# Spectral pieces beside the selective scan: transfers issued by ScalarE in the place of SyncE, four columns mixed in one piece, at most four pieces a step

## The chip, the cores and the metric

The kernel runs on one core of one Trainium2 chip. The metric is the device time of one execution in microseconds; the time of the kernel before is the median of three runs. The profile is of one further execution.

Engine names are those of the profile: PE is the matrix engine (TensorE), PEld its weight loads, DVE is VectorE, ACT is ScalarE, POOL is GpSimd, SP is SyncE, which only issues transfers here. PEclk is the clock that was granted to PE, as a share of full speed.

## The reference

The input x is (8, 64, 64, 96): eight images of 64 × 64 positions with 96 channels, in 32-bit floats. Four residual layers follow one another; each normalizes its input in groups of three channels over the whole image and adds its result to x:

```python
x = x + L0(_gn(x))   # selective scan: 4 orders of the 4096 positions, 192 channels, 16 states each
x = x + L1(_gn(x))   # chunked scan of the same 4 orders with one decay per head
x = x + L2(_gn(x))   # selective scan as L0, with other weights
x = x + L3(_gn(x))   # spectral layer
```

The core of a selective scan is, per position of an order,

```python
h = h * exp(dt * A) + (dt * u) * b      # 192 channels x 16 states
y = sum_n(h * c)
```

The spectral layer raises the image to 128 × 128 with a low-pass filter, applies to each of the 16384 positions a hidden layer of 384 with the polynomial c0 + c1·h + c2·h², comes back to 96 channels, filters again and keeps every second row and column. The filters are separable, so the kernel writes them as products with the matrices `up` (64 to 128) and `down` (128 to 64), first along one direction, then along the other.

## The kernel before

**The images.** A loop goes over the eight images. For each, L0, L1 and L2 are computed one after the other with `project`, the scan and `back`. The spectral layer of an image needs little of DVE and POOL, so it isn't computed at its own place but in small pieces beside the two selective scans of the next image: the first half beside L0's, the second half beside L2's. The first image has no pieces beside it. The last image's spectral layer is done at the end in `spectral_layer`, which the change does not touch. So 14 of 16 selective scans have pieces beside them.

**The scan.** `selective_scan` goes over 32 steps (four orders of eight chunks of 512 positions). A step has six units t, n = t % 6; a unit is 32 channels × 4 states on the partitions and four groups of states along the free axis. The order of all instructions is written out by hand (`manual_schedule`): each engine and each transfer queue takes its instructions in the order in which the program issues them. For one unit:

- `spread` (L834, PE): `pu`, the channels of dt·u repeated over the partitions, into the one buffer `misc`;
- `with_b` (L840): `db` = pu · b, on DVE; for n = 2 and 5 on POOL instead, from the loaded `du2`;
- `decays(t, p)` (L855, ACT): `da` = exp(dt · A), half p of the unit into one of two buffers, which is free again only when the scan of the same half of the unit before has read it;
- `scan(t, p)` (L870, DVE): the recurrence over half p, into `h`;
- `leave` (L886 ACT, L891 POOL): the last state is copied out, then h is multiplied by c in place. `enter` (L826, ACT) puts the state where the scan three units on starts from;
- `total_y` (L898 and L908, PE): sums h over its states into `py`, for the units 0 to 2 of a step in unit 3, for 3 to 5 in unit 0 of the next step; ACT copies the sums to y (L993 in unit 4, L1007 in unit 1).

`prepare` works up to two steps ahead: it makes dt, b, c and du of a chunk (PE L742 and L751, ACT L747, L755 and L775, POOL L793 or L799), writes them to DRAM and loads them back repeated over partitions (`bcd`, `dd`, `dud`, `dx`, `b`, `c`, `du2`). All these transfers are issued by SP.

**The pieces.** `slow_layer` makes two lists of pieces. A piece is a tuple (load, norm, matmuls, evacuation, store, lead). The three kinds are:

- `rows(j)`, 16 of two pieces: normalize and turn four rows, then multiply by `up` and store to `x1d`. One load of `xs` (the tile sx) serves two j.
- `cols(n)`, 32 of seven pieces: load four columns of x1d (the tile sc), multiply by `up` (`down_h`, `fine` L509); three times `hidden` and `square` (L516, L523); two `mix` pieces of two columns each (L532 and L536, evacuated by `mixed` L547); `lower` (L555, L564) and a store to `g2d`.
- `ends(j)`, 16 of one piece: load `xr` (the tile sr, once for two j) and `g2` (the tile s) from g2d, add the bias (`shift`, L588), multiply by `down`, add the residual (L592 and L601), evacuate (`done`, L611), store to the output.

The first list has the rows, two empty places and the columns 0 to 14: 139 places. The second has the columns 15 to 31, two empty places and the ends: 137.

**Beside.** The class `Beside` puts the lists into the scan. `begin` issues a piece's matmuls into a PSUM buffer that it shares with total_y and prepare (`py`) or with spread (`misc`). `end` issues the evacuation on ACT, then the loads that are due, and the `norm` of the next piece. A store isn't issued by `end` but kept in `waiting`, and `flush` issues it when the next piece has begun. A load is issued when the piece before its own is next, at the earliest. All loads and stores of the pieces go through SP, in the order of the program, between those of `prepare`.

Each step has a quota: list length times step number over 32, rounded down, less the same for the step before; here four or five pieces. The text calls the places in a step A to E: A begins and ends in unit 1, B begins at the start of unit 2 and ends in its middle, C begins there and ends at the unit's end, D lies in the first half of unit 4, E at the start of unit 5.

Of the kernel before, what the change touches and what calls it, by code (L numbers as in the profile page):

```python
# [17 lines left out]
DM = 96  # L18
# [49 lines left out]
def tile_vision_stack(  # L68
# [19 lines left out]
    nc = tc.nc  # L88
# [55 lines left out]
    w2q, b1q, coefq = hidden_parts(w3bs)  # L144
# [288 lines left out]
    def slow_layer(prev):  # L433
# [12 lines left out]
        def rows(j):  # L446

            def load():
                if j % 2 == 0:
                    live["xs", j] = xs = wide("sx")[:DM]  # L450
                    nc.sync.dma_start(xs, xd[:, j * 256 : j * 256 + 512])

            def norm():
                if j % 2 == 0:
                    live["xn"] = xn = wide("sn")[:DM]
                    nc.scalar.activation(
                        xn, live["xs", j], AF.Identity, scale=sb[:, 0:1], bias=sb[:, 1:2]
                    )

            def turn(ps):  # L460
                pt = ps[:64, : 4 * DM].rearrange("p (i c) -> p i c", i=4)
                for i in range(4):
                    at = (j % 2) * 256 + 64 * i
                    nc.tensor.transpose(pt[:, i, :], live["xn"][:, at : at + 64], ident[:DM, :DM])

            def turned(ps):
                live["xt"] = xt = narrow("st", "g")
                nc.scalar.copy(xt[:64].rearrange("p i c -> p (i c)"), ps[:64, : 4 * DM])

            def across(ps):  # L470
                nc.tensor.matmul(
                    ps[:, : 4 * DM],
                    up,
                    live["xt"][:64].rearrange("p i c -> p (i c)"),
                    start=True,
                    stop=True,
                )

            def crossed(ps):
                live["x1"] = x1 = wide("sw")[:, : 4 * DM]  # L480
                nc.scalar.copy(x1, ps[:, : 4 * DM])

            def store():
                nc.sync.dma_start(
                    x1d[4 * j : 4 * j + 4].rearrange("h w c -> w h c"),
                    live["x1"].rearrange("p (h c) -> p h c", h=4),
                )

            return [(load, norm, turn, turned, None, 4), (None, None, across, crossed, store, 0)]

        def cols(n):

            def load():
                live["c1"] = c1 = narrow("sc", "x1")[:64]
                nc.sync.dma_start(c1, x1d[:, 4 * n : 4 * n + 4])

            def down_h(ps):
                for i in range(4):
                    nc.tensor.matmul(
                        ps[:DM, i * 128 : i * 128 + 128],  # L500
                        live["c1"][:, i, :],
                        up,
                        start=True,
                        stop=True,
                    )

            def fine(ps):
                live["x2"] = x2 = wide("s2")[:DM]
                nc.scalar.copy(x2, ps[:DM])  # L509
                live["f"] = []  # L510

            ops = [(load, None, down_h, fine, None, 4 if n else 0)]
            for m in range(3):

                def hidden(ps, m=m):
                    nc.tensor.matmul(  # L516
                        ps, w3as[:, m * 128 : (m + 1) * 128], live["x2"], start=True, stop=True
                    )

                def square(ps, m=m):  # L520
                    f = wide("sf")
                    live["f"].append(f)
                    nc.scalar.activation(f, ps, AF.Square, bias=b1q[:, m : m + 1])  # L523

                ops.append((None, None, hidden, square, None, 0))
            for p in range(2):

                def mix(ps, p=p):
                    for i in range(2):
                        at = (2 * p + i) * 128  # L530
                        po = ps[:, i * DM : i * DM + DM]
                        nc.tensor.matmul(  # L532
                            po, live["x2"][:, at : at + 128], w12, start=True, stop=False
                        )
                        for m in range(3):
                            nc.tensor.matmul(  # L536
                                po,
                                live["f"][m][:, at : at + 128],
                                w2q[:, m, :],
                                start=False,  # L540
                                stop=(m == 2),
                            )

                def mixed(ps, p=p):
                    if p == 0:
                        live["g"] = narrow("sg", "g")
                    nc.scalar.copy(  # L547
                        live["g"][:, 2 * p : 2 * p + 2, :].rearrange("p i c -> p (i c)"),
                        ps[:, : 2 * DM],
                    )  # L550

                ops.append((None, None, mix, mixed, None, 0))

            def lower(ps):
                nc.tensor.matmul(  # L555
                    ps[:64, : 4 * DM],
                    down,
                    live["g"].rearrange("p i c -> p (i c)"),
                    start=True,
                    stop=True,  # L560
                )

            def lowered(ps):
                nc.scalar.copy(  # L564
                    live["g"][:64].rearrange("p i c -> p (i c)"), ps[:64, : 4 * DM]
                )

            def store():
                nc.sync.dma_start(
                    g2d[4 * n : 4 * n + 4].rearrange("w h c -> h w c"), live["g"][:64]  # L570
                )

            ops.append((None, None, lower, lowered, store, 0))
            return ops

        def ends(j):

            def load():
                if j % 2 == 0:
                    live["xr", j // 2] = xr = wide("sr")[:DM]  # L580
                    nc.sync.dma_start(xr, xd[:, j * 256 : j * 256 + 512])
                live["g2", j] = g2 = narrow("s3", "g" if j % 2 else "x1")
                nc.sync.dma_start(g2, g2d[:, 4 * j : 4 * j + 4])

            def shift():
                if j % 2 == 0:
# [24 lines left out]
                nc.scalar.copy(res, ps[:64, : 4 * DM])  # L611

            def store():
                nc.sync.dma_start(
                    dst[:, 4 * j : 4 * j + 4, :],
                    live["res"].rearrange("p (h c) -> p h c", h=4),
                )
# [11 lines left out]
    class Beside:  # L629

        def __init__(self, ops):
            self.ops, self.at, self.waiting, self.loaded = ops, 0, None, 0
            self.open = None
            if ops:
                self.load(0)
                self.prepare(0)
                self.ahead(0)
# [14 lines left out]
            if k < len(self.ops) and self.ops[k] and self.ops[k][1]:  # L652
                self.ops[k][1]()

        def flush(self):
            if self.waiting:
                self.waiting()
                self.waiting = None

        def begin(self, pool, tag):  # L660
            if self.at >= len(self.ops):
                return
            op = self.ops[self.at]
            if op:
                ps = pool.tile([128, LC], F32, name="ps", tag=tag)
                op[2](ps)
                self.flush()
                self.open = (op, ps)
            else:
                self.flush()  # L670
                self.open = (None, None)

        def end(self):
            if not self.open:
                return
            op, ps = self.open
            self.open = None
            if op:
                op[3](ps)
                self.waiting = op[4]  # L680
            self.at += 1
            if self.loaded <= self.at < len(self.ops):
                self.flush()
                while self.loaded <= self.at:
                    self.load(self.loaded)
            self.prepare(self.at)
            self.ahead(self.at)


    def selective_scan(w, wdt, a, d, u, y, beside):  # L690
# [23 lines left out]
        with (  # L714
# [248 lines left out]
            with tc.tile_pool(name="p_da", bufs=1, space=PSUM) as pap:  # L963
# [12 lines left out]
                for t in range(total + 2):  # L976
# [2 lines left out]
                    quota = (i + 1) * len(ops) // len(steps) - i * len(ops) // len(steps)  # L979
                    if n == 2 and quota > 1:  # L980
                        other.begin(pyp, "py")
                    elif n == 5 and quota > 4:
                        other.begin(pmp, "misc")
                    if n in (0, 3, 5) and ahead:
                        spread(t + 1)
                    elif n == 1 and t + 2 < total:
# [5 lines left out]
                    elif n == 4:  # L992
# [1 line left out]
                        if quota > 3:  # L994
                            other.begin(pmp, "misc")
                        prepare_part(i + 2)
                    if n == 5:
                        other.end()
                    if t < total:
                        scan(t, 0)  # L1000
                        if n % 3 == 0 and t + 2 < total:
# [28 lines left out]
                        other.end()  # L1030
                    if n in (0, 1, 5):
                        prepare_part(i + 1)
                other.flush()
                assert other.at == len(ops)

    def chunked_scan(w, wd, d, u, y):
# [735 lines left out]
```

## Time and profile before

| | |
|---|---|
| runs | 27078.75, 27082.73, 27084.66 us; median 27082.73 |
| profiled execution | 27082.74 us; its span 27080.9 us |
| busy: PE, DVE, ACT, POOL | 22624.0, 23966.2, 16539.7, 21781.7 us |
| mean granted PE clock | 0.773 |
| transfers, queue of SP | 2807.32 MB, 41.9% of 16 engines' span |
| transfers, queue of ACT | 6.29 MB, 0.1% |
| scans of DVE (L870) | 6144, 2282 ns each |
| products of POOL (L891) | 3072, 4174 ns each |
| half mixes evacuated (L547) | 448, 317 ns each |

Times in the profile are counted from the start of the span. Lines of groups give the line, the engine, the operation and the names of what is written and read, then the count, the busy time with the mean of one, and the idle time of the engine before them with what ended most of it. Lines of the timeline give the start, the duration, the engine and line, the operation and the count, and in brackets the idle time before and what ended it. Lines of windows give the stretch, its length, the busy time and count of each engine, the granted clock, the share of the transfer engines and GB/s. A busy time is a mean over stages with different limits.

### The profile page before, as it was taken

How to read it: one execution, taken by the hardware profiler on the slowest of the kernel's cores; microseconds unless marked ns; L12 is line 12 of the kernel's file. 1: busy time of each engine (PE TensorE's matmuls, PEld its weight loads, DVE VectorE, ACT ScalarE, POOL GpSimd, SP SyncE). 2: the span in 40 equal slices, each digit the busy share in tenths (PEclk: the TensorE clock that was granted, in tenths of full speed). 3: DMA queues.
4: the chain of work that ended last, by engine and by line, in shares of the span. 5: the costliest groups of instructions: out<-in, count | busy, mean ns of one | idle time of the engine just before them, and what ended most of it. 6: DMA issues, size and time to landing. Idle time of an engine off the chain costs nothing. (4 is left out here: it accounts for less than half of the span.)

```text
span 27080.9 us, 283056 instructions
## 1 busy us (share of the span) xinstructions
PE 22624.0 (84%) x91061; PEld 8150.5 (30%) x91061; DVE 23966.2 (88%) x17105; ACT 16539.7 (61%) x29953; POOL 21781.7 (80%) x8360
## 2 busy tenths in 40 slices
PE   7787788888888888888888888888888888888888
PEld 2141122422224222242222422224222342223424
DVE  8989899798997989979898898988989889898896
ACT  5656566466665656556565565655656556565564
POOL 8949898498984979859797697976979769797694
PEclk7687777877778777787777877778777787778878
DMA  4415454154541545415453254532545325453252
GB/s 121 119 30 124 114 130 117 31 131 122 132 111 35 133 117 137 103 44 132 116 136 98 50 132 118 135 92 56 133 119 134 85 62 133 118 134 78 70 133 67
DMA packets 1681704, 2831.72 MB, mean 105 GB/s; under 512 B 434984, under 2 KB 478280, under 8 KB 1675616
## 3 DMA queue, kind: packets, MB, share of 16 engines
q1 hardware_dynamic: 1663584, 2807.32, 41.9%
q8 instruction: 730, 11.96, 0.2%
q10 hardware_dynamic: 16640, 6.29, 0.1%
q14 instruction: 750, 6.14, 0.1%
HBM read 2385.11 MB, written 427.49 MB: 104 GB/s over the span
## 5 line engine op out<-in xcount | busy, mean ns | idle before, releaser
L870 DVE TENSOR_TENSOR_SCAN h<-da,db 128x1026 f32<-128x1026 f32 x6144 | 13765.8, 2282 | 900.6 <-ACT da L855 479.2
L891 POOL TENSOR_TENSOR h<-h,c 128x2048 f32<-128x2048 f32 x3072 | 12769.4, 4174 | 726.0 <-ACT state L886 510.1
L908 PE MATMUL py<-h,cst 128*32 128x512 f32 x24576 | 5301.4, 795 | 69.9 <-POOL h L891 69.8
L855 ACT ACTIVATE da<-dx,a2s 128x512 f32<-128x512 f32 x6144 | 4236.4, 690 | 1508.7 <-DVE h L870 1366.6
L855 ACT ACTIVATE da<-dx,a0s 128x512 f32<-128x512 f32 x6144 | 4235.8, 690 | 1481.8 <-DVE h L870 1344.3
L840 POOL TENSOR_TENSOR db<-du,b 128x2048 f32<-128x2048 f32 x1024 | 4648.2, 4539 | 567.6 <-ACT db L826 567.6
L840 DVE TENSOR_TENSOR db<-pu,b 128x2048 f32<-128x2048 f32 x2048 | 4643.9, 2268 | 110.9 <-PE pu L834 100.6
L834 PE MATMUL pu<-du,cst 32*128 32x512 f32 x4096 | 3239.2, 881 | 1007.4 <-DVE db L840 799.9
L908 PEld LDWEIGHTS py<-h,cst 128*32 128x32 f32 x24576 | 1175.0, 142 | 4827.3 <-issue 4517.4
L751 PE MATMUL pv<-u,wk 96*128 96x512 f32 x2048 | 1816.9, 1030 | 688.4 <-ACT raw L747 685.8
L898 PE MATMUL py<-y,cst 96*96 96x512 f32 x1536 | 1517.0, 1084 | 397.9 <-ACT raw L755 395.4
L834 PEld LDWEIGHTS pu<-du,cst 32*128 32x128 f32 x4096 | 790.4, 239 | 3079.7 <-issue 1361.9
L742 PE MATMUL pv<-u,wk 96*96 96x512 f32 x2048 | 1452.4, 838 | 186.7 <-ACT y L993 142.6
L1285 ACT ACTIVATE sg<-sg 128x768 f32<-128x768 f32 x1024 | 819.6, 800 | 859.1 <-PE sg L1269 859.1
L993 ACT COPY y<-py 96x512 f32<-96x512 f32 x512 | 417.5, 815 | 1411.4 <-PE py L908 1411.4
L516 PE MATMUL ps<-s,w3as 96*128 96x512 f32 x1344 | 912.4, 767 | 327.7 <-ACT sf L523 188.1
L1239 POOL TENSOR_TENSOR ce<-ec,cr 112x512 f32<-112x512 f32 x256 | 530.8, 2074 | 719.1 <-ACT ec L1237 700.8
L1317 DVE TENSOR_TENSOR wt<-wt,cbm 128x768 f32<-128x768 f32 x1024 | 985.3, 997 | 136.6 <-ACT wt L1286 136.1
L886 ACT COPY state<-h 128x4 f32<-128x4 f32 x3072 | 597.5, 194 | 782.5 <-DVE h L870 776.8
L751 PEld LDWEIGHTS pv<-u,wk 96*128 96x128 f32 x2048 | 540.6, 291 | 1740.2 <-ACT raw L747 1212.5
L319 POOL TENSOR_SCALAR xn<-xs,sb 96x512 f32<-96x512 f32 x192 | 198.1, 1033 | 991.7 <-PE pz L324 495.6
L1216 POOL TENSOR_TENSOR rr<-lr,cc 128x768 f32<-128x768 f32 x256 | 376.6, 1471 | 754.1 <-ACT lr L1214 749.2
(241 smaller groups left out, 30790.9 us busy)
## 6 DMA issues: line engine op xcount, KB each, us to landing
dx<-dd SPq DMA_DIRECT2D x4096, 192.0 KB
b<-bcd SPq DMA_DIRECT2D x2048, 256.0 KB
c<-bcd SPq DMA_DIRECT2D x2048, 256.0 KB
du<-dud SPq DMA_DIRECT2D x2048, 128.0 KB
dd<-raw SPq DMA_DIRECT2D x1024, 192.0 KB
dud<-du SPq DMA_DIRECT2D x512, 128.0 KB
xd<-xs SPq DMA_DIRECT2D x256, 192.0 KB
cr<-bcd SPq DMA_DIRECT2D x1536, 32.0 KB
```

What stands on the lines that cost most here:

```text
L516: nc.tensor.matmul(ps, w3as[:, m * 128 : (m + 1) * 128], live["x2"], start=True, stop=True)
L742: nc.tensor.matmul(pv[:DM], weights[k][:, hi, 128:], uv[hi], start=(hi == 0), stop=(hi == 1))
L751: nc.tensor.matmul(pv, weights[k][:, hi, :128], uv[hi], start=(hi == 0), stop=(hi == 1))
L834: nc.tensor.matmul(pu, sel[rows, :], m["du"][rows, n // 3, :], start=True, stop=True)
L840: (nc.gpsimd if pool else nc.vector).tensor_mul(groups(m["db", n]), (m["du2"][:, n // 3, :] if pool else m["pu"]) .unsqueeze(1) .to_broadc ...
L855: nc.scalar.activation(dst[:, g, :LC], made[i]["dx"][n // 3][:, n % 3, :], AF.Exp, scale=av4[:, k, n, gs : gs + 1],)
L870: nc.vector.tensor_tensor_scan(made[i]["h", n][:, at][:, way], das[p][:, rev : 2 * SEG + rev][:, way], made[i]["db", n][:, at][:, way], 0. ...
L891: nc.gpsimd.tensor_mul(h, h, made[i]["c"])
L898: nc.tensor.matmul(py, skip[:, hf, :] if k == 0 else ident[:DM, :DM], view((u if k == 0 else y)[:, hf, :], wh, c * LC, LC), start=True, st ...
L908: nc.tensor.matmul(py[32 * q : 32 * q + 32, :], red, hs[q][:, g, :], start=False, stop=(g == NSG - 1),)
L1285: nc.scalar.activation(sg, sg, AF.Abs)
L1317: nc.vector.tensor_mul(it["wt"], it["wt"], m["cbm"][:, j : j + 1, :].to_broadcast([128, RK, Q]),)
```

## The change

Three things are changed, all of them in the pieces and where they are put:

1. The seven kinds of transfers of the pieces are issued by ACT (`nc.scalar.dma_start`) in the place of SP. A store is issued directly behind its evacuation; `waiting` and `flush` are gone.
2. The two `mix` pieces of a column group become one: 16 matmuls of the program in the place of 8 and 8, and one evacuation of 384 columns in the place of two of 192. `cols(n)` has six pieces, so the lists have 124 and 120 places.
3. With these lengths the quota is three or four, and the place E is taken out of the loop of the scan.

```diff
             def load():
                 live["c1"] = c1 = narrow("sc", "x1")[:64]
-                nc.sync.dma_start(c1, x1d[:, 4 * n : 4 * n + 4])
+                nc.scalar.dma_start(c1, x1d[:, 4 * n : 4 * n + 4])
...
-            for p in range(2):
-
-                def mix(ps, p=p):
-                    for i in range(2):
-                        at = (2 * p + i) * 128
-                        po = ps[:, i * DM : i * DM + DM]
+            def mix(ps):
+                for i in range(4):
+                    at = i * 128
+                    po = ps[:, i * DM : i * DM + DM]
+                    nc.tensor.matmul(
+                        po, live["x2"][:, at : at + 128], w12, start=True, stop=False
+                    )
+                    for m in range(3):
                         nc.tensor.matmul(
-                            po, live["x2"][:, at : at + 128], w12, start=True, stop=False
+                            po,
+                            live["f"][m][:, at : at + 128],
+                            w2q[:, m, :],
+                            start=False,
+                            stop=(m == 2),
                         )
...
+            def mixed(ps):
+                live["g"] = narrow("sg", "g")
+                nc.scalar.copy(live["g"].rearrange("p i c -> p (i c)"), ps[:, : 4 * DM])
...
-        def flush(self):
-            if self.waiting:
-                self.waiting()
-                self.waiting = None
...
         def end(self):
...
             if op:
                 op[3](ps)
-                self.waiting = op[4]
+                if op[4]:
+                    op[4]()
             self.at += 1
-            if self.loaded <= self.at < len(self.ops):
-                self.flush()
-                while self.loaded <= self.at:
-                    self.load(self.loaded)
+            while self.loaded <= self.at < len(self.ops):
+                self.load(self.loaded)
             self.prepare(self.at)
             self.ahead(self.at)
...
-                    elif n == 5 and quota > 4:
-                        other.begin(pmp, "misc")
...
-                    if n == 5:
-                        other.end()
```

The other transfers (`sx`, `x1d`, `g2d`, `sr`, `s`, the output) change in the same way as the one shown.

## The prediction

> **What bounds the kernel now.** I read the page first, for the engines and the two costliest groups.
>
> ```profile
> span 27080.9 us, 283056 instructions
> PE 22624.0 (84%) x91061; PEld 8150.5 (30%) x91061; DVE 23966.2 (88%) x17105; ACT 16539.7 (61%) x29953; POOL 21781.7 (80%) x8360
> L870 DVE TENSOR_TENSOR_SCAN h<-da,db 128x1026 f32<-128x1026 f32 x6144 | 13765.8, 2282 | 900.6 <-ACT da L855 479.2
> L891 POOL TENSOR_TENSOR h<-h,c 128x2048 f32<-128x2048 f32 x3072 | 12769.4, 4174 | 726.0 <-ACT state L886 510.1
> ```
>
> No engine is full on average, so I went to the stage that the change touches: 16 scans of 32 steps, 14 of them with spectral pieces beside. One step needs 12 scans and 4 products of VectorE (12 × 2.24 + 4 × 2.27 = 36.0 us) and, on GpSimd, 6 × 4.17 + 2 × 4.54 + 2.35 to 2.9 = 36.5 us. The starts of successive steps in the timeline are on average 37.4 us (columns in the first scan) and 37.2 us (in the second) apart, the shortest 36.25. Both engines are therefore nearly full, and a step grows when ACT or TensorE, which feed both, is late. Windows cut at two steps show it:
>
> ```profile
> 3837.40:3875.61 38.21, 35.09 (x105) 11.85 (x104) 35.72 (x17) 25.81 (x48) 38.21 (x10) 0.72 0.53 130
> 3913.46:3949.81 36.35, 32.71 (x112) 11.14 (x111) 35.60 (x17) 25.83 (x48) 34.36 (x9) 0.78 0.52 127
> ```
>
> (Length, then PE, weight loads, DVE, ACT, POOL, clock, DMA.) The first step, 38.21 us, has its mixes in slots C and D; the second, 36.35 us, has them in A and B. Slots: A begins and ends in unit 1, B and C share unit 2, D lies in unit 4, E at the start of unit 5. The timeline of the first step, slots C and D:
>
> ```profile
> 3853.96 0.74 PE L532 MATMUL ps<-w,s 96*128 96x96 f32 x2 [0.79 <-ACT sf L523]
> 3856.20 1.49 PE L536 MATMUL ps<-w3bs,sf 128*128 128x96 f32 x6
> 3857.62 2.07 PE L834 MATMUL pu<-du,cst 32*128 32x512 f32 x2
> 3857.72 0.32 ACT L547 COPY sg<-ps 128x192 f32<-128x192 f32 x1 [2.32 <-PE ps L536]
> 3860.40 2.27 DVE L840 TENSOR_TENSOR db<-pu,b 128x2048 f32<-128x2048 f32 x1
> 3866.48 1.07 ACT L993 COPY y<-py 96x512 f32<-96x512 f32 x1 [4.35 <-PE py L908]
> ```
>
> Half a column group's mix runs from 3853.96 to 3857.69, 3.73 us; ACT stands 2.32 us for it; the spread (L834) queued behind it on TensorE ends at 3859.69, only 0.71 us before VectorE's product takes it. In the second step the same piece takes 2.03 us in slot A (3925.95 to 3927.98), and again in B:
>
> ```profile
> 3925.95 0.46 PE L532 MATMUL ps<-w,s 96*128 96x96 f32 x2 [0.45 <-ACT state L886]
> 3927.15 0.83 PE L536 MATMUL ps<-w3bs,sf 128*128 128x96 f32 x6
> 3928.02 0.32 ACT L547 COPY sg<-ps 128x192 f32<-128x192 f32 x1 [0.72 <-PE ps L536]
> 3930.66 0.20 ACT L886 COPY state<-h 128x4 f32<-128x4 f32 x1
> ```
>
> The granted clock is why (the figure after the bracket):
>
> ```profile
> 3853.96:3857.69 3.73, 3.73 (x17) 0.50 1.03 224
> 3924.00:3929.00 5.00, 4.14 (x29) 1.00 0.62 152
> ```
>
> The waits add up what the present pieces cost ACT (total us, times, longest):
>
> ```profile
> ACT sg L547 <- PE ps L536: 404.6, 343, 3.3
> ACT sr L588 <- DMA sr<-xd: 168.8, 21, 11.1
> ACT sn L456 <- DMA sx<-xd: 153.1, 21, 8.6
> ```
>
> **The change, part by part.**
>
> *Slots.* A column group has six pieces instead of seven, so the first list falls from 139 to 124 and the second from 137 to 120. Over 32 steps that is at most four each; slot E goes. In the column steps VectorE's idle time is 1.4 us with four pieces and 2.5 (first scan) or 2.0 us (second) with five. These steps are in the mean that I compare with.
>
> *Transfers.* By the counts in the DMA list 56+112+224+224+56+112+112 = 896 issues move from SP to ACT, 128 a batch. ACT's own rows are the 16 issues of tok, 427 to 606 ns, while SP issued too; SP's medians for the moved ones are 347 to 623 ns. At those medians they sum to 64 us of ACT a batch. In the first two rows on ACT the next instruction starts 0.03 us after the issue ends, so I count each in line: 0.46 us for a column load, 0.7 us for a column store (0.62 and the wait for ACT's own copy). Queued behind them on ACT are da, the state copy and, through these, both full engines. Bounds: 0 (alongside other work) to 1.3 us, a c load's issue in a busy burst at 4041.6 (nine in ten take 0.43 or less). SP gets those slots free; its waiting consumers were those of sx, sr and, with 98 us, of the g2d loads.
>
> *The merged mix.* Two halves become one: 2 × 2.02 = 4.04 us at full clock, 2 × 3.73 = 7.46 us at half. Pairing the new lists with the slots gives, per batch, 8 mixes in A, 9 in B, 8 in C, 7 in D. Steps without a stall last 36.55 us; times below count from the step's start, as measured in the two steps above.
> - A: TensorE from 12.49 to 16.53; copy 0.47 and load 0.46 to 17.5; da 1.41 to 19.0, 0.55 late for unit 3's first scan; the next piece's copy and store put the state copy at 20.2 in place of 17.2, and unit 3's second scan 0.6 late. 36.55 + 1.2, and a little for GpSimd, whose product is 3 us late but which has 2 to 4 us of backlog: 38.0.
> - B: TensorE from 14.65 to 18.7, copy and load to 19.7, da to 21.4 against 20.9: 37.1.
> - C: TensorE from 16.56 at half clock to 24.0; spread to 26.1, when VectorE wanted it at 23.0: 3.1 us, and 0.35 for the tail: 40.0.
> - D: steps with half a mix there and a slow total_y last 38.1; TensorE 2.0 us and the load 0.5 longer, less 0.4 that scans cover: state and da 2.0 us later in the one place where no product of VectorE lies between: 40.1.
> - The other 18 column steps lose E: 37.15.
>
> Against 37.3: 8 × 0.7 − 9 × 0.2 + 8 × 2.7 + 7 × 2.8 − 18 × 0.15 = 42.3 us a batch; × 7 batches = +296 us.
>
> That the clock stays at half for all of C is read from the trace: it is 0.50 from 3853.7 to 3863.9, though TensorE works throughout. TensorE: Matmul & The Clock Gate (Part 1, What's actually happening) has it back at full rate after one busy window of about 3.4 us. By that page a C mix would end about 1.8 us sooner, an estimate, and the whole sum would be about 100 us smaller; the row decides.
>
> *Rows.* Steps 3 to 5 of the first scans last 38.9 us where sx is late (issued at 3588.85 behind c loads, its reader starts at 3596.29). On ACT the load comes in D and its reader one slot on, in A of the next step, 20 us later: the wait goes, −1.4 × 3 us. Norm and store now both lie in A: + 0.1 × 7. About −25 us in all (bounds −60 and +20).
>
> DMA: Bandwidth & Descriptors (Issuing engines are not separate DMA queues) says that the issuing engine changes only the sequencer's time, since all share 16 DMA engines. No run here shows ACT and SP loads side by side under this load; by that page alone sx and sr would land no sooner.
>
> *Ends.* Step 28 of the second scans lasts 49.65 us, since ACT stands 11 us at shift for a load that SP issued late. ACT would now issue sr itself, in C, where da has over 3 us: 39.5, −10 us. In the next three steps three or four issues a slot cost +1 us each. −7 × 7 = −50 us (bounds −90 and +30).
>
> Sum: 296 − 25 − 50 = +221. The profiled execution took 27082.74 us, 0.01 from the median 27082.73, with a span of 27080.9: 27,300 us.
>
> **Rivals.**
> - *Cover holds (faster).* GpSimd's backlog hides A and B, TensorE gets to full clock in C, and issues run beside other work. Then only the gains are left: E's idle time, 63 × 1.06 + 49 × 0.49 + 14 × 0.47 = 97 us, rows 27 and ends 70: 26,890. For it: mixes in A and B now stand in the fastest steps. It decides from the point at which the mix in C ends 4.4 us after its start (3.73 + 0.71) and that in D 2.8 us after; no row has a merged mix, so this is open. Against it: in C half the work already takes 3.73 us.
> - *Heavier (slower still).* The single long mix leaves the clock at half in A and B too, + 2.5 us each: 17 × 2.5 × 7 = 298 us: 27,600. Against it: 1.00 in the second step.
> - *The transfers bring nothing.* The move is made, but sx and sr land as late: rows and ends keep their time: 27,380.
>
> **How the numbers follow.** Forecast 0.60, cover holds 0.21, heavier 0.14, transfers nothing 0.05. Lower bound of the forecast's own terms: issues at 0 take off 100 us, ends 40: 27,160; with C 100 us short as well, 27,060. Upper: issues at 1.3 us add 175 us, ends 80: 27,560. I give 27,060 to 27,620, which takes in the heavier rival; what is left out is the faster part of the first rival, 0.17, and some 0.03 above. A difference of 0.2% is 54 us, about what a measurement can tell. Faster by more: 0.17, from the first rival. Within: 0.11 (0.04 of the first rival, 0.07 of the forecast with short waits). Slower: 0.72 (0.53 of the forecast, 0.14 and 0.05).
>
> **What would show it.** In the profile after: 224 copies of 128x384 on ACT behind L536, with about 700 to 900 us of wait against 404.6; C mixes of 7 us or more at clock 0.5 and db (L840) waiting for pu; column steps of 40 us where the mix lies in C or D; no wait for sx, step 28 near 39.5 us; issues on ACT of 0.4 to 0.7 us. Wrong, if a C mix ends within 4.4 us, or if steps with a mix in C or D stay below 38.5 us.

## The result and the profile after

The changed kernel takes 27,318.9 us (median of four runs, 27,302.7 to 27,327.9), the kernel before 27,082.9 us: a ratio of 1.0087, 95% interval 1.0069 to 1.0104. It is slower by 236 us. The forecast was 27,300 us. The sum was close, but two of its three terms were wrong, by 129 and 120 us and in opposite directions. The profiled execution has a span of 27,325.5 us, 244.6 us more than before.

The page first. DVE and POOL do what they did; the idle time ahead of DVE's scans rose from 900.6 to 1105.0 us, with da the main releaser as before (479.2 before, 682.6 now).

```profile
span 27325.5 us, 282265 instructions
PE 22865.0 (84%) x91061; PEld 8264.2 (30%) x91061; DVE 23999.4 (88%) x17105; ACT 16529.0 (60%) x29729; POOL 21778.4 (80%) x8360
L856 DVE TENSOR_TENSOR_SCAN h<-da,db 128x1026 f32<-128x1026 f32 x6144 | 13794.6, 2283 | 1105.0 <-ACT da L841 682.6
L877 POOL TENSOR_TENSOR h<-h,c 128x2048 f32<-128x2048 f32 x3072 | 12752.0, 4175 | 724.8 <-issue 399.3
```

(Lines have moved: the scan is L856, POOL's product L877, da L841, spread L820, db L826, the merged evacuation L544, shift L582.)

As in the prediction, a step runs from the start of its first scan to the start of the next step's. Summed by part, after less before, in us over the seven images:

| part | forecast | measured |
|---|---|---|
| rows (steps 0 to 8 of the first scans) | -25 | -25 |
| columns (9 to 31 of the first, 0 to 26 of the second) | +296 | +167 |
| ends (27 to 31 of the second) | -50 | +70 |
| outside the scans | 0 | +32 |
| sum | +221 | +244 |

By slot of the merged mix, the column steps came out as follows (mean over the seven images):

| mix in | steps an image | forecast | measured |
|---|---|---|---|
| A | 8 | 38.0 | 38.1 (36.8 to 38.7) |
| B | 9 | 37.1 | 37.1 (36.2 to 38.3) |
| C | 8 | 40.0 | 38.7 (36.4 to 43.0) |
| D | 7 | 40.1 | 38.2 (37.1 to 38.8) |
| none | 18 | 37.15 | 37.26 (36.3 to 38.0) |

(In brackets, the shortest and the longest step of the slot, each a mean over the images.) C is not one case but two. Windows cut at two steps that both have their mix in C (steps 14 and 25 of the same scan), and at the two mixes themselves, with the columns length, PE, weight loads, DVE, ACT, POOL, clock, DMA, GB/s:

```profile
7343.99:7380.40 36.41, 30.07 (x107) 10.13 (x106) 35.64 (x16) 26.15 (x48) 36.41 (x10) 0.83 0.52 134
7756.23:7798.36 42.13, 38.85 (x107) 14.15 (x106) 35.94 (x17) 26.01 (x48) 38.05 (x10) 0.66 0.40 103
7360.42:7364.24 3.82, 3.81 (x33) 3.72 (x33) 3.72 (x2) 1.42 (x4) 3.82 (x2) 1.00 0.01 3
7772.83:7779.99 7.16, 7.14 (x33) 6.97 (x33) 6.44 (x3) 1.43 (x4) 7.16 (x3) 0.50 0.01 2
```

The same matmuls take 3.8 us at full clock and 7.1 at half. In the step at half clock the first half went as foretold for C, as the timeline of that step shows (start, duration, engine and line, in brackets the idle time before):

```profile
7772.85 0.74 PE L530 MATMUL ps<-w,s 96*128 96x96 f32 x2 [0.79 <-ACT sf L523]
7778.51 1.49 PE L534 MATMUL ps<-w3bs,sf 128*128 128x96 f32 x6
7779.92 2.07 PE L820 MATMUL pu<-du,cst 32*128 32x512 f32 x2
7780.03 0.48 ACT L544 COPY sg<-ps 128x384 f32<-128x384 f32 x1 [5.74 <-PE ps L534]
7780.04 0.46 ACTq L495 DMA_DIRECT2D sc<-x1d  x1
7782.03 2.29 DVE L826 TENSOR_TENSOR db<-pu,b 128x2048 f32<-128x2048 f32 x1 [2.66 <-PE pu L820]
7788.81 1.02 ACT L977 COPY y<-py 96x512 f32<-96x512 f32 x1 [5.33 <-PE py L894]
7791.13 2.29 DVE L856 TENSOR_TENSOR_SCAN h<-da,db 128x1026 f32<-128x1026 f32 x1 [2.23 <-ACT da L841]
```

ACT stands 5.74 us for the mix, the spread queued behind it ends at 7782.0, and DVE's product is 2.66 us late (forecast 3.1). Then comes a second wait, which the forecast had at 0.35 us: the sums over the states (L894) also end late, ACT stands 5.33 us for them, and DVE 2.23 us for the da behind. So the step is 42.13 us long and not 40.0.

But only 26 of the 56 mixes in C ran at half clock, none of those in A and D, and 3 of 63 in B (those for most of their 6.2 to 6.3 us). In C the steps at half clock last 41.6 us on average, those at full clock 36.3. The 30 mixes at full clock cost nothing: step 14, at 36.4 us, is nearly as short as the shortest step (36.25 us). The same step of different images shows it too: step 23 of the second scans has its mix at half clock in six images (41.3 to 41.4 us) and at full clock in one (36.25 us).

The waits of ACT (total us, times, longest):

```profile
ACT sg L544 <- PE ps L534: 608.9, 224, 5.7
ACT sr L582 <- DMA sr<-xd: 46.4, 14, 5.1
ACT sn L456 <- DMA sx<-xd: 12.3, 7, 1.9
ACT da L841 <- DMA dx<-dd: 104.5, 27, 8.0
```

The waits for sr and sx are down from 168.8 and 153.1 us. The fourth line is new: ACT now waits for dx, a transfer that the change does not touch. Why it is late is seen in the waits of SP, which no longer issues any transfer of the pieces and yet waits for them to land:

```profile
SPq L750 <- DMA sc<-x1d: 1496.3, 98, 18.2
SPq L750 <- DMA g2d<-sg: 1007.1, 98, 13.8
SPq L768 <- DMA sc<-x1d: 821.2, 112, 11.4
SPq L768 <- DMA out_dram<-so: 297.3, 28, 13.8
```

(L750 issues b and c, L768 dx.) SP's waits for landings of the pieces' transfers add up to 5,057 us, against 45 before. The trace gives the reason. Each transfer signals a semaphore, a counter that others can wait on, when it has landed. This program has eight of them for its transfers (99 and 101 to 107), given out in turn over all transfers whichever engine issues them, and a transfer is issued only when the one that had its semaphore last has landed. As long as SP issued nearly all of them, that was one queue waiting for its own past. Now SP's load can be held by a transfer that ACT issues only when it gets there. In step 29 of a second scan the fourth load of dx and an output store share semaphore 105:

```profile
9893.71 13.91 SPq L768 DMA_DIRECT2D dx<-dd  x4
9904.97 0.64 ACTq L608 DMA_DIRECT2D out_dram<-so  x1
9905.65 0.61 ACTq L575 DMA_DIRECT2D sr<-xd  x1
9910.87 1.42 ACT L841 ACTIVATE da<-dx,a2s 128x512 f32<-128x512 f32 x2 [5.92 <-DMA bcd<-raw]
9912.31 2.29 DVE L856 TENSOR_TENSOR_SCAN h<-da,db 128x1026 f32<-128x1026 f32 x1 [3.55 <-ACT da L841]
```

The waits of SP in a window around this step (9885 to 9935 us) name the store:

```profile
SPq L768 <- DMA out_dram<-so: 11.9, 1, 11.9
```

SP issues three loads of dx, stands 11.9 us for a store that ACT issues at 9904.97, and issues the fourth at 9907.32. The da that reads dx starts at 9910.87, though ACT was ready at 9906.7, and DVE loses 3.55 us. (The line of da names the landing of bcd. But the semaphores on which ACT waits last ahead of this da are 105 and 102, and bcd signals 106; the fourth load of dx completes 105 at 9910.76. So it is dx.)

### The profile page after: what moved, and what is told of

Read it like the earlier page. It is cut to its first block, busy times and chain, and to the rows that moved or that the text cites. A ratio compares the mean times of both kernels' runs of the same rounds, so it can differ in the third digit from the quotient of the medians.

```text
span 27325.5 us, 282265 instructions
## 1 busy us (share of the span) xinstructions
PE 22865.0 (84%) x91061; PEld 8264.2 (30%) x91061; DVE 23999.4 (88%) x17105; ACT 16529.0 (60%) x29729; POOL 21778.4 (80%) x8360
## 5 line engine op out<-in xcount | busy, mean ns | idle before, releaser
L856 DVE TENSOR_TENSOR_SCAN h<-da,db 128x1026 f32<-128x1026 f32 x6144 | 13794.6, 2283 | 1105.0 <-ACT da L841 682.6
L877 POOL TENSOR_TENSOR h<-h,c 128x2048 f32<-128x2048 f32 x3072 | 12752.0, 4175 | 724.8 <-issue 399.3
L894 PE MATMUL py<-h,cst 128*32 128x512 f32 x24576 | 5414.6, 801 | 112.3 <-POOL h L877 111.8
L826 POOL TENSOR_TENSOR db<-du,b 128x2048 f32<-128x2048 f32 x1024 | 4650.6, 4542 | 800.1 <-ACT db L812 571.3
L841 ACT ACTIVATE da<-dx,a2s 128x512 f32<-128x512 f32 x6144 | 4231.2, 689 | 1495.4 <-DVE h L856 1127.4
L841 ACT ACTIVATE da<-dx,a0s 128x512 f32<-128x512 f32 x6144 | 4231.8, 689 | 1361.4 <-DVE h L856 1185.3
L826 DVE TENSOR_TENSOR db<-pu,b 128x2048 f32<-128x2048 f32 x2048 | 4644.1, 2268 | 92.0 <-PE pu L820 84.7
L820 PE MATMUL pu<-du,cst 32*128 32x512 f32 x4096 | 3293.5, 895 | 778.2 <-DVE db L826 735.6
L894 PEld LDWEIGHTS py<-h,cst 128*32 128x32 f32 x24576 | 1254.5, 142 | 4901.2 <-issue 4096.4
L820 PEld LDWEIGHTS pu<-du,cst 32*128 32x128 f32 x4096 | 801.7, 243 | 3012.4 <-DVE db L826 1245.5
```

The lines of the kernel that those rows point to most:

```text
L820: nc.tensor.matmul(pu, sel[rows, :], m["du"][rows, n // 3, :], start=True, stop=True)
L826: (nc.gpsimd if pool else nc.vector).tensor_mul(groups(m["db", n]), (m["du2"][:, n // 3, :] if pool else m["pu"]) .unsqueeze(1) .to_broadc ...
L841: nc.scalar.activation(dst[:, g, :LC], made[i]["dx"][n // 3][:, n % 3, :], AF.Exp, scale=av4[:, k, n, gs : gs + 1],)
L856: nc.vector.tensor_tensor_scan(made[i]["h", n][:, at][:, way], das[p][:, rev : 2 * SEG + rev][:, way], made[i]["db", n][:, at][:, way], 0. ...
L877: nc.gpsimd.tensor_mul(h, h, made[i]["c"])
L894: nc.tensor.matmul(py[32 * q : 32 * q + 32, :], red, hs[q][:, g, :], start=False, stop=(g == NSG - 1),)
```

## The experiments

All are compared with runs of the kernel before on the same chip; ratios have their 95% interval. The table splits each profiled span into the parts used above, less the kernel before's, in us; "none" are the two scans without pieces, and "rest" is what lies outside the scans. The splits are of one profiled execution each, whose total can differ from the median that the ratio goes by.

| kernel | ratio | rows | columns | ends | none | rest |
|---|---|---|---|---|---|---|
| changed | 1.0087 [1.0069, 1.0104] | -25 | +167 | +70 | 0 | +32 |
| transfers alone | 1.0056 [1.0043, 1.0070] | -13 | +187 | +17 | 0 | +23 |
| merge alone | 1.0015 [1.0006, 1.0024] | -42 | +166 | -73 | +2 | +32 |
| merge, copies on ACT | 1.0024 [1.0015, 1.0033] | -39 | +191 | -62 | -1 | +48 |
| ends on SP | 1.0052 [1.0040, 1.0065] | -29 | +184 | -12 | 0 | -7 |
| merge, useless transfers | 1.0067 [1.0054, 1.0081] | -37 | +177 | +62 | 0 | +24 |
| merge, mixes in B and D | 0.9984 [0.9975, 0.9993] | -38 | +131 | -105 | 0 | -13 |
| the same, filler in scans without pieces | 0.9953 [0.9941, 0.9966] | -42 | +83 | -111 | -56 | -28 |
| the same, filler in light places | 0.9961 [0.9948, 0.9973] | -52 | +89 | -93 | -56 | -2 |
| the same, filler in every A | 0.9962 [0.9949, 0.9976] | -53 | +71 | -94 | -55 | +5 |
| changed, filler in every A | 1.0132 [1.0115, 1.0149] | -24 | +276 | +116 | 0 | -18 |

### The two halves of the change

Transfers alone: the kernel before with

```diff
-                nc.sync.dma_start(c1, x1d[:, 4 * n : 4 * n + 4])
+                nc.scalar.dma_start(c1, x1d[:, 4 * n : 4 * n + 4])
...
-                self.waiting = op[4]
+                if op[4]:
+                    op[4]()
```

and the same for the other six transfers.

> Part 1 of the change alone: the seven kinds of transfers on ACT, stores directly behind their evacuations; half mixes and the five slots as before. Theory M (the merged mix costs everything; the transfers only take waits away, those for sx and sr): 27,000 to 27,080 us, steps 28 to 31 of the second scans shorter than before in sum (162.8 us). Theory T (the transfers cost too: SP's loads of dx, b and c for the next steps wait behind transfers that ACT issues only when it gets to them, and ACT itself spends the issues in line): about 27,200 us, +70 from the ends, -20 from the rows, +60 from issues in line in the column steps; steps 28 to 31 of the second scans about 170 us in sum; waits of SP for landings of sc, sg and so in the list, which the kernel before does not have.

Merge alone: the kernel before with the merged `mix` and without the slot E; transfers, `waiting` and `flush` as they were.

> Parts 2 and 3 alone: merged mix, 124 and 120 places, at most four a step; all transfers on SP with the held-back stores, as before. Theory M: 27,360 us or more (the whole +236 and the gain of sx and sr lost). Theory T: about 27,140 us: +130 from the four C mixes per image that run at half clock (steps 25, 28 and 31 of the first scans, 23 of the second), about -70 from the fifth slot that is gone; ends as before, within 2 us a scan.

Theory M falls. The transfers alone cost 0.56%, the merge alone 0.15%; together 0.71%, within the interval of the whole change. That agreement is chance: part by part the two do not add up (columns +187 and +166 apart and +167 together, ends +17 and -73 apart and +70 together). The move is the larger half either way: 0.56% by itself, 0.72% on top of the merge.

The merge alone has a column term of the same size (+166, as the changed kernel has +167), but not in the same steps. The steps 25 and 28 that I had expected to be long took 36.4 us. At half clock, wholly or mostly, ran the mixes of step 31 of the first and 7 and 23 of the second scans (21 in C), and 16 of the 63 in B. The merge alone also has gains in rows and ends that I had put down to the transfers: with 124 and 120 places the loads of sx and sr come early enough from SP. No wait of sn for sx is in its list, and of the wait for sr this is left:

```profile
ACT sr L582 <- DMA sr<-xd: 112.2, 14, 9.9
```

Of my numbers, the ends of the merge were missed (I had "within 2 us a scan"; they fell by 10). For the transfers alone, rows (-20 foretold) and the sum of the last four steps (164 us, between the two theories) came out close; its columns are dearer than foretold (+187 against +60; what makes the difference was not separated), and its SP waits 5,220 us for landings of the pieces.

So the move of the transfers, added to the merge, costs 17 us in the rows and 144 in the ends, and in the columns nothing net.

### Is it ACT's time or SP's waits?

Copies on ACT: in the merge alone, at each place where the changed kernel issues a transfer,

```diff
+        def idle(n):
+            t = pool[0].tile([128, 128], F32, name="idle", tag="idle", bufs=1)
+            for at in range(0, 128, 128 // n):
+                nc.scalar.copy(t[:DM, at : at + 128 // n], w3as[:, at : at + 128 // n])
```

> The merge alone with transfers on SP, and on ACT, at each place where the changed kernel issues a transfer, copies of a constant about as long as the issue (one of 128 columns for a column load, two of 64 for the stores and the loads of sx and sr), written to a tile that nobody reads. If ACT's time for the issues is what the transfers cost, it takes what the changed kernel takes, 27,320 us, less the 35 us that sx and sr gain: about 27,300 to 27,350, with ends of 170 us. If it is SP's loads that wait, it stays within 60 us of the merge alone.

It stayed near the merge alone: 1.0024 against 1.0015, with intervals that overlap, and ends of 11 us more, not 144. The copies took 369 us of ACT in all, the issues of the changed kernel 468 us, so they are somewhat short; but even scaled up they come nowhere near 144 us. ACT's time for issues isn't the price in the ends. One thing the copies don't imitate: a column store waits for the evacuation ahead of it, and da and the state copy behind it stood 142 us for that in the changed kernel.

Useless transfers: in the merge alone, behind each evacuation of an end, three times

```diff
+            nc.scalar.dma_start(live["idle"][:16, 2 * k : 2 * k + 2], xd[:16, 2 * k : 2 * k + 2])
```

> The merge alone (all transfers on SP), and behind each evacuation of an end three tiny loads issued by ACT into a tile that nobody reads (16 rows of 8 bytes each). Nothing waits for their data, and ACT spends about 1.4 us on them per end, less than the filler copies did. Theory of the shared semaphores (a transfer that SP issues must wait until the transfer eight places before it in the program has landed, and that may be one that ACT issues only later): SP's list shows waits for landings of idle, steps 28 to 31 of the second scans rise from 149 to 160 us or more, +70 to +150 us in all. Rival (ACT's time): +10 to +25 us, no such waits.

1.0067 against 1.0015: steps 28 to 31 rose from 149 to 168 us. Bytes that nobody reads cost the ends 135 us, about what the real transfers cost. The waits of SP for them:

```profile
SPq L615 <- DMA idle<-xd: 111.5, 24, 6.3
SPq L765 <- DMA idle<-xd: 65.0, 21, 8.8
SPq L787 <- DMA idle<-xd: 48.8, 7, 7.8
```

And the timeline of ACT in step 28 of a second scan of the same kernel:

```profile
9890.21 0.47 ACT L610 COPY so<-ps 64x384 f32<-64x384 f32 x1 [5.24 <-PE ps L600]
9890.22 3.93 ACTq L573 DMA_DIRECT2D idle<-xd  x3
9896.86 0.72 ACT L587 ACTIVATE sr<-sr,b2q 96x512 f32<-96x512 f32 x1 [6.18 <-DMA idle<-xd]
```

It goes both ways: SP waits for ACT's transfers to land, and ACT's three issues, 0.43 us each in the median, take 3.93 us, since they in turn wait for transfers of SP: the second has semaphore 101 after a load of c from SP, and starts 0.02 us after that load's landing. (The line of shift, L587, names idle too, but the last of its semaphores to be reached is 106, that of SP's load of sr.) With the copies and this run together, the theory of the shared semaphores is shown for the ends, as far as it can be without a kernel in which they are not shared; that was not tried.

Ends on SP: the changed kernel with `sr`, `s` and the output back on SP, stores held back.

> The changed kernel with only the transfers of the ends (sr, s, output) put back on SP, their stores held back as before; rows and columns stay on ACT. If the ends' transfers on ACT are what the ends cost: steps 28 to 31 of the second scans 149 us in sum as in the merge alone (after: 171), and about 140 us less than the changed kernel, some 0.3% above the kernel before. If the ends are long for another reason (more of them in a step): within 30 us of the changed kernel.

Steps 28 to 31 fell to 148.6 us, as foretold, but step 27 rose from 38.4 to 49.3: SP, still held up by the transfers of the columns, issues the first sr late. Its loads of b wait 12.0 us there for the landing of a g2d store of ACT, and sr, behind them in SP's queue, is issued at 9829.15.

```profile
9836.61 0.72 ACT L582 ACTIVATE sr<-sr,b2q 96x512 f32<-96x512 f32 x1 [17.62 <-DMA sr<-xd]
```

So only about 80 of the foretold 140 us came back in the ends: with the columns on ACT and the ends on SP, each queue still waits for the other's transfers.

### What the mix costs where

Mixes in B and D: the merge alone with

```diff
-        gap = [None, None]
-        first = flat(rows(j) for j in range(16)) + gap + flat(cols(n) for n in range(SPLIT))
-        second = flat(cols(n) for n in range(SPLIT, 32)) + gap + flat(ends(j) for j in range(16))
+        gap = [None]
+        first = flat(rows(j) for j in range(16)) + 3 * gap
+        first += flat(cols(n) for n in range(SPLIT)) + 3 * gap
+        second = gap + flat(cols(n) for n in range(SPLIT, 32)) + 5 * gap
+        for j in range(16):
+            second += ends(j) + (gap if j in (2, 5, 8, 11) else [])
```

> The merge alone (transfers on SP), but with empty places put into the lists so that both have 128 places, four in every step, and each mix falls into B or D; the ends are spread over the last six steps with an empty place after every third. If only mixes in C cost time, since only there the clock is at half: 26,950 to 27,020 us, no mix above 3.9 us. If my prediction's price of D (2.8 us a step) is right: 16 mixes in D an image, +310 us against the kernel before's column steps, 27,300 us or more.

At 0.9984 it is faster than the kernel before, but by less than foretold. D is not as dear as I had it: its steps last 38.4 us. And B is not safe: of 112 mixes in B, 25 ran mostly at half clock there (6.2 to 6.7 us), so "only C" was wrong. Most of the gain is in the ends, although step 26 of the second scans waits for the first sr (43.7 us).

Changed, filler in every A: the changed kernel with one product that nobody reads ahead of the piece in A:

```diff
+                            idle = pyp.tile([128, LC], F32, name="ps", tag="py")
+                            nc.tensor.matmul(idle, w3as[:, :128], u[:, 0, :LC], start=True, stop=True)
```

> The changed kernel as it is, with one product of 128 x 512 whose result nobody reads ahead of the piece in A in every step with pieces. If the long steps of the changed kernel's columns (25, 28 and 31 of the first scans with 42.1, 43.0 and 38.0 us, 23 of the second with 40.6) are long because TensorE's clock is at half for the mix in C, all mixes take 3.8 us and these steps fall to 38 us or less: about -13 us a pair of scans; what the product costs in the other steps is open (0 to +0.3 us each, since the last kernel with it gave back what it gained). Total between 70 us less and 30 us more than the changed kernel. If the clock is not the cause: the mixes at 3.8 us and the steps still at 40 us or more.

In the three steps with a mix that it was made for it is right: 25, 28 and 23 fall from 42.1, 43.0 and 40.6 to 37.7, 37.8 and 36.3 us. The window of the step that was 42.13 us:

```profile
7806.46:7844.20 37.74, 33.77 (x109) 10.51 (x108) 35.82 (x16) 26.13 (x48) 37.38 (x11) 0.82 0.47 123
```

The clock is 0.82 in place of 0.66, with more work for PE. But step 31's mix still ran at half, in all seven images. In the first scans the mixes in A came 1.6 us later, and their steps went from 38.4 to 41.6 us. The total, 1.0132 against 1.0087, missed the foretold range. The clock is the cause of the long steps in C; one more product is no remedy.

### A faster version

Filler in scans without pieces: mixes in B and D, the load of the first end three places earlier, and in the two scans without pieces three products in the place of A.

```diff
-            return [(load, shift, last, done, store, 1 if j else 0)]
+            return [(load, shift, last, done, store, 1 if j else 3)]
...
+                        if t < total and not ops:
+                            idle = pyp.tile([128, LC], F32, name="ps", tag="py")
+                            for m in range(3):
+                                nc.tensor.matmul(
+                                    idle, w3as[:, m * 128 : (m + 1) * 128], u[:, 0, :LC],
+                                    start=True, stop=True,
+                                )
```

> The kernel with mixes in B and D, with the load of the first end issued three places earlier, and, in the two scans that have no pieces beside them, three matrix products of 128 x 512 a step in the place of A whose result nobody reads. If the steps without pieces last 37.5 us because TensorE's clock falls to half between the two sums over the states (total_y then ends late and ACT stands for it), the products keep the clock up and these steps fall to about 36.4 us: -70 us; the load takes step 26 of the second scans from 43.7 to about 37.5 us: -40 us. In all about 110 us under the kernel with mixes in B and D, 0.6% under the kernel before. Rival (more work for TensorE is only in the way): these steps 37.5 us or longer.

0.9953 [0.9941, 0.9966], the fastest here beside the next two, which don't differ from it. One step without pieces (step 12 of the first scan) in the kernel before, as a window:

```profile
573.99:611.54 37.55, 28.95 (x69) 6.47 (x68) 35.71 (x17) 24.20 (x44) 36.63 (x10) 0.68 0.54 128
```

And the timeline of its middle, with the waits in brackets:

```profile
596.62 5.70 PE L908 MATMUL py<-h,cst 128*32 128x512 f32 x24
602.43 1.05 ACT L993 COPY y<-py 96x512 f32<-96x512 f32 x1 [3.59 <-PE py L908]
604.77 2.29 DVE L870 TENSOR_TENSOR_SCAN h<-da,db 128x1026 f32<-128x1026 f32 x1 [0.81 <-ACT da L855]
```

The sum over the states takes 5.70 us, ACT waits for it and DVE for ACT. The same step with the filler, first the window:

```profile
563.92:600.51 36.59, 30.00 (x75) 7.13 (x74) 35.60 (x17) 24.47 (x44) 36.59 (x10) 0.73 0.58 139
```

Then its timeline, where L1006 is the filler:

```profile
576.67 2.84 PE L1006 MATMUL ps<-u,w3as 96*128 96x512 f32 x6
585.48 4.49 PE L905 MATMUL py<-h,cst 128*32 128x512 f32 x24
590.08 1.03 ACT L988 COPY y<-py 96x512 f32<-96x512 f32 x1 [1.35 <-PE py L905]
```

Idle work took 28 us off each of the two scans; DVE's wait is gone in this step. The foretold fall of step 26 came as well (43.7 to 37.4).

Filler in light places and in every A: the last kernel, where the number of products now depends on the piece (three for an empty place, two ahead of a product of the rows or an end; in the second kernel one ahead of every other piece).

```diff
-                        if t < total and not ops:
+                        m = other.light()
+                        if t < total and m:
...
-                            for m in range(3):
+                            for m in range(m):
```

Neither changes the total in a way that can be measured.

> The last kernel (mixes in B and D, first end's load earlier, filler products in the scans without pieces) with filler products also ahead of the piece in A where that is light: three where the place is empty, two ahead of a product of the rows or an end. If the half clock is what holds the steps of the rows at 37.5 us (steps 3 to 8 of the first scans), they fall to about 36.5: -45 us; the ends by 0 to 1 us a step, -20 us. About 26,910 us, 0.7% under the kernel before. Rival: in the rows ACT or the transfers hold them, and nothing changes.

The steps of the rows (3 to 8) went from 37.5 to 37.3 us only, not to 36.5: what holds them was not found.

> As the kernel with filler in light places, and one more filler product ahead of every other piece in A. If it keeps the clock up for the mixes in B that still run at half (6.2 to 6.6 us: step 20 of the first scans, 7 and 22 of the second), these three steps fall by 3 us each: -60 us. Rival: the product puts the pieces in A and B 1.1 us later, which costs in the 48 other column steps more than the three gain: up to +100 us.

All 224 mixes ran at full clock and the three steps fell by 2 to 3 us (39.6, 40.3 and 40.3 to 37.5, 37.4 and 37.4), but the other column steps gave back most of it: the columns went from +89 to +71 us, where three steps of seven images had gained about 55.

## Why the prediction was right, and where it was wrong

- *Columns, +296 foretold, +167 measured.* A, B and the steps without a mix were right to 0.1 us as means; the single steps of A and B lie up to 1.2 us off, so that is luck in part. The step that failed is "C: TensorE from 16.56 at half clock to 24.0", taken for all eight: one window of one step stood for a slot. The trace before had it already: of its 105 half mixes in C, 44 ran wholly at half clock and 49 wholly at full. Where the clock was at half, the working holds up to the spread; "0.35 for the tail" was too small (2.23 us of wait in step 25), and the steps last 41.6 us on average. Where it was full, half the cases, "cover holds" was right, with its own condition: the mix ends 3.8 us after its start, below the 4.4 of that rival. The mean of C is 38.74, 1.26 less, and 8 × 1.26 × 7 = 71 us. D, "40.1", was mis-sized: 38.2, that is 7 × 1.9 × 7 = 93 us. The mix in D does hold up da (1.62 us of DVE's time in one such step, 17 of a first scan, where 2.0 were foretold), so it is the 38.1 that this was added to that no longer held; why was not separated. The rest goes the other way: 14 from the steps without a mix, 5 from A, and 16 since the steps before were 37.25 us on average where I had put 37.3 (50 × 0.046 × 7); 296 - 71 - 93 + 35 = 167.
- *The clock rule.* In step 25 the trace has PE busy without a break from 7772.85 on and the clock at 0.50 for 13.65 us, from 7772.66. The rule in the Trainium skill, TensorE: Matmul & The Clock Gate (Part 1, What's actually happening), that the clock is back after one busy window of about 3.4 us, does not fit that, as far as busy time in the profile, where the ends of matmuls are modelled, is what the rule means by busy. My row (half for all of C) was right on that, wrong on how often. Nor was PE idle for long before the fall: the idle times ahead of the last hidden products and the mix are 0.8 to 0.9 us each.
- *Issues on ACT.* Foretold 0.4 to 0.7 us; the medians are 0.47 for sc, 0.64 for g2d, 0.61 for sr, 0.62 for the output, and less for sx (0.33) and x1d (0.37). Their price on the path was too high: copies nearly as long cost 0.09% with overlapping intervals and 25 us in the columns, where I had 100 us for the columns alone. That SP's queue could be held by them I had not seen: I wrote that "SP gets those slots free".
- *Rows, -25 foretold, -25 measured, for another reason.* The wait for sx went, but it goes without the move too, and by more (-42 in the merge alone).
- *Ends, -50 foretold, +70 measured.* Step 28 came to 39.7 us (39.5 foretold). The step that failed is "+1 us each" for the next three: 44.8, 44.5 and 42.1 in place of 39.2, 39.8 and 34.2, that is +5.6, +4.7 and +7.9. Step 27, by then with an end in it, adds 1.9. Its bounds reached +30. The copies and the useless transfers show the missing term: transfers of ACT and SP wait for each other.
- *The signs of being wrong.* I had put down two: a C mix that ends within 4.4 us, and steps with a mix in C or D below 38.5 us. Both came true in part: 30 of 56 C mixes took 3.8 us, and the mean of D is 38.2. ACT's wait for the mix, 608.9 us, lies below the 700 to 900 that I gave. So the total within its range does not confirm the working.
- *The rivals.* "Heavier" (half clock in A and B): none of 56 in A, 3 of 63 in B. "The transfers bring nothing": ACT's waits for sx and sr are nearly gone, so as stated it is wrong. I had priced the issues on ACT, but not that the move makes SP wait, and the move is the larger half of the loss. What I took from the Trainium skill, DMA: Bandwidth & Descriptors (Issuing engines are not separate DMA queues), that issuing from several engines saves only the sequencer's time, says too little for this program: ACT's wait for sr is 46.4 us with ACT's issue against 112.2 in the merge alone, and useless transfers on ACT cost 0.5%.
- *Outside the scans, +32, not foretold.* These stretches vary from -28 to +48 us between the kernels; no run here tells why.

The forecast of 27,300 us is near by luck: 129 us too much in the columns and 120 too little in the ends nearly cancelled.

## What to carry to other kernels

Before moving transfers to another engine's queue, look up what each queue waits for beyond its data: where semaphores are shared in turn, a prefetching queue is tied to the pace of the engine that got the transfers, and the list of waits of that queue shows it at once. A cost read from one window at half clock has to be compared with every place where the piece lies; the same matmuls took 3.8 or 7.1 us. Try the parts of a change alone: here the gain that looked like the transfers' came with the shorter lists. And when the parts do not add up, an agreement of the totals shows nothing.

## What the runs showed of the hardware

The granted clock has two values in these traces, 1.00 and 0.50, and changes in steps of 3.41 us: the stretches are multiples of that, most often 6.83 or 10.24 us at full and 10.24 or 13.65 at half in the changed kernel. In the scans without pieces it goes through 6.83 at full, 10.24 at half, 6.83 at full, 13.65 at half, 37.55 us in all, and the step takes 37.5 us too, 1.2 us more than the shortest steps. With three idle products a step the first stretch at full is mostly 10.24 us long in place of 6.83, and the steps fall to 36.2 to 37.2 us. Whether the step follows the clock or the clock the step was not separated, but work that keeps TensorE busy shortened the step though the result is thrown away.
